# A hybrid of convolution, attention and scan: ScalarE's instructions of the first stage in program order, relus and scaled rows dealt out over the next attention, weight factors moved to the products

## Chip, cores and metric

The kernel runs on one core of one Trainium2 chip, as one program. The metric is the device time of one execution in microseconds (us), as the median of several runs. The engines are called PE (TensorE), ACT (ScalarE), DVE (VectorE), POOL (GpSimd) and SP (SyncE, whose queue issues the DMAs). All data is in 32-bit floats.

## What is computed

The input is x of 4 images, 128 channels, 64 x 64 pixels. Layer 0 is a normalisation by groups and a hybrid of three convolutions and an attention over all pixels; layer 1, over the same data as 4 x 4096 tokens, is a two-way scan (Mamba, heads of 64, chunks of 64) and a recurrent network. The change touches layer 0 alone.

```python
def hybrid(x):                       # layer 0, on v = _gn(input); input + hybrid(v)
    x7 = conv2d(x, w7, b7, 3)        # 7x7, 128 -> 128 channels
    x5 = conv2d(x, w5, b5, 2)
    x3 = conv2d(x, w3, b3, 1)
    theta, phi, g = conv1x1(x, ...)  # 64 channels each, hw = 4096 pixels
    attn = softmax(einsum('bcn,bcm->bnm', theta, phi) / sqrt(64))
    xn = conv1x1(einsum('bcm,bnm->bcn', g, attn), ow, ob) + x
    return relu(x7 + x5 + x3 + xn + x)
# layer 1, on tokens t of layer 0's output
t = t + mamba_forward(_ln_t(t)) + mamba_backward(_ln_t(t))
t = t + recurrent(_ln_t(t))
```

## The kernel before

The function `conv_attention` is the first stage, up to about 1745 us of the profiled span; the second stage (scan and recurrent network) follows. The three convolutions and the residual are one 7x7 convolution, whose weights are added up on the chip (`weights`). It is done by a fast algorithm in both directions: along a row each three taps become two-point forms (`forms`: sums and differences of neighbouring pixels, L325, into tiles `yf`, with one set of weights for sums, one for differences), and down the rows the seven taps of an image's rows split into eight parts m = 0 to 7, at the points 0, plus and minus U = 0.75, plus and minus V = 1.5, and the rest. `transform(m)` (L291 to L310) combines rows of the padded image `xp` into `yx` (with `yb` for help) for m below 6; m = 1, 2 and m = 3, 4 are pairs that share `yb` and the first tile's products. For parts 0 to 5 there are three groups of products (n = 0, 1, 2), for 6 and 7 two. The weights of parts 0 to 5 are made once, at the start, and stored in DRAM as `wd`, three for each part; each group loads its own (`wt<-wd`, 2 buffers, L364), while the middle weights stay in `wc`.

One step n = 8 b + q (32 in all) has an attention and then one part of a convolution of image b. The attention of step n is over 512 queries of the image against its 4096 keys, in eight turns. A turn issues the scores of the next two key tiles (`scores`: four matmuls L421 into a pf tile, two pf tiles of PSUM, then one exp L423 of 128 x 1024 each into one of four `ex` buffers) and then the values of the present two (`values`: L432 on PE, and on DVE the running sum of exponentials `es`, L436 for the first and L438 for the others). After the eighth turn comes `convolve`, one part in the order

```python
ORDER = (1, 2, 0, 6, 7, 5, 3, 4)   # images 0 to 2
LAST = (1, 2, 3, 4, 6, 7, 5, 0)    # image 3
```

Each group of products goes through PSUM tiles `pm` (L351) to `eo`: ACT copies one half (L369), DVE makes sum and difference (L371) and adds the outer products (L374), POOL adds the base of group 0 (L380). Then the results go into the image rows of `t`: for m = 2 by POOL (L386, L387) and three scaled rows on ACT (L388 to L390); for m = 4 by POOL's u and four-row updates on DVE (L398); otherwise by POOL (L403). The matmul `den` (L442) sums es over the partitions, between the groups of products. In the first step of the next image, `finish(b)` goes over the image before in eight parts: load of the untouched input as `xr` (L459, 2 buffers), relu with bias on ACT (L461), addition on POOL (L462). At the last step of an image the convolution is interleaved with the keys of the next (`keys`, L263 to L276), and three steps before its end DVE takes the next image's statistics (`bn_stats`). At the end of each convolution but the last, `queries` (L410, L412) makes the theta of the next step.

The order on PE is the program's (`manual_schedule`); on ACT, DVE, POOL and SP the framework's scheduler orders instructions by its own cost estimates. Each engine runs its instructions strictly in the order that results. The making of weights is spread over steps 0, 1 and 2: `thirds` (from L494), `pair(1)`, `single(0)`, `single(5)`, `pair(3)`, with ACT, DVE and POOL taking part and rows of 128 x 1152.

Of the kernel before, what the change touches and what calls it, by code (L numbers as in the profile page):

```python
# [10 lines left out]
F32 = mybir.dt.float32  # L11
AF = mybir.ActivationFunctionType
ALU = mybir.AluOpType
# [3 lines left out]
P = 128  # L17
# [136 lines left out]
def conv_attention(nc, tc, k, a, t, B, H, W, flags, load, mem, loads):  # L154
# [18 lines left out]
    NQ = T // NC  # L173
    RW = NC // W
    XT = 2 * NC
    KB, PC = H // 4, W // 2
# [5 lines left out]
    U, V = 0.75, 1.5  # L182
    UU, VV = U * U, V * V

    with ExitStack() as ctx:
        wp = ctx.enter_context(tc.tile_pool(name="l0_w", bufs=1))
        wc = wp.tile([P, 9, P], F32, name="wc")
# [10 lines left out]
        yx = wp.tile([P, KB + 1, WP], F32, name="yx")  # L198
        yb = wp.tile([P, KB + 1, WP], F32, name="yb")
        yd = wp.tile([P, KB, WP], F32, name="yd")  # L200
# [27 lines left out]
        ctx.enter_context(tc.manual_schedule(engines={mybir.EngineType.PE}))  # L228
# [58 lines left out]
        def every(j, n):  # L287

            return xp[:, j : j + 4 * n - 3 : 4, :]

        def transform(m):  # L291

            row = lambda j: every(j, KB + 1)
            if m in (0, 5):
                j = m // 5
                nc.scalar.mul(yx, row(j + 2), -(UU + VV))
                nc.scalar.mul(yb, row(j), UU * VV)
                nc.gpsimd.tensor_tensor(yx, yx, row(j + 4), ALU.add)
                nc.gpsimd.tensor_tensor(yx, yx, yb, ALU.add)
            elif m in (1, 3):  # L300
                nc.scalar.mul(yb, row(1), -(VV if m == 1 else UU))
                nc.gpsimd.tensor_tensor(yb, yb, row(3), ALU.add)
                nc.scalar.mul(yx, row(2), -(VV if m == 1 else UU))
                nc.gpsimd.tensor_tensor(yx, yx, row(4), ALU.add)
                nc.scalar.mul(yb, yb, U if m == 1 else V)
                nc.gpsimd.tensor_tensor(yx, yx, yb, ALU.add)
            else:

                nc.scalar.mul(yb, yb, -2.0)
                nc.gpsimd.tensor_tensor(yx, yx, yb, ALU.add)  # L310

        def forms(m):

            def both(rows, g):
                v = rows.rearrange("p (k g) c -> p k g c", g=2)[:, :, g]
                f = fm.tile([P, 4, KB // 2, PC + 2], F32, tag="yf", name="yf", bufs=4)  # L320
                at = lambda j: v[:, :, j : j + 2 * PC + 3 : 2]
                for kx, (x, y, op) in enumerate(
                    ((0, 2, ALU.subtract), (1, 2, ALU.add), (2, 1, ALU.subtract), (3, 1, ALU.subtract))
                ):
                    nc.gpsimd.tensor_tensor(f[:, kx], at(x), at(y), op)  # L325
                return v, f

            if m >= 6:
                return [None] + [[both(every(m - 2, KB), g)] for g in range(2)]
            transform(m)  # L330
            out = [[both(yx[:, 0:KB], 1)]]
            nc.gpsimd.tensor_tensor(yd, yx[:, 0:KB], yx[:, 1 : KB + 1], ALU.subtract)
            for g in range(2):
                out.append([both(yd, g)])
                if m in (0, 5):
                    out[-1].append(both(every(3 + 3 * m // 5, KB), g))
            return out
# [16 lines left out]
        def convolve(b, m, f):  # L354
# [3 lines left out]
            for n in range(3):  # L358
# [10 lines left out]
                nc.scalar.copy(eo[:, 1, :], pm[:, 1, :])  # L369
                for e, op in enumerate((ALU.add, ALU.subtract)):  # L370
                    nc.vector.tensor_tensor(eo[:, e, :], pm[:, 0, :], eo[:, 1, :], op)  # L371
                yield
                pm = products(fn, (0, 3))
                nc.vector.tensor_tensor(eo, eo, pm, ALU.add)  # L374
# [10 lines left out]
                elif m == 2:  # L385
                    nc.gpsimd.tensor_tensor(out(0), in_(mid[n]), in_(eo), ALU.add)  # L386
                    nc.gpsimd.tensor_tensor(mid[n], mid[n], eo, ALU.subtract)  # L387
                    nc.scalar.mul(out(2), out(0), UU)  # L388
                    nc.scalar.mul(out(1), in_(mid[n]), U)
                    nc.scalar.mul(out(3), in_(mid[n]), U * UU)  # L390
# [65 lines left out]
        def finish(b):  # L456
            for q in range(NQ):
                xr = wk.tile([P, NC], F32, tag="xr", name="xr")
                nc.sync.dma_start(xr, image_in(b)[:, bass.ts(q, NC)])  # L459
                r = t[:, ds(b * T + q * NC, NC)]  # L460
                nc.scalar.activation(r, r, AF.Relu, bias=bsum)  # L461
                nc.gpsimd.tensor_tensor(r, r, xr, ALU.add)  # L462

# [16 lines left out]
        def weights():  # L480
# [13 lines left out]
            def thirds(g, new):  # L494

                ac = free[:, 0 : new.shape[1], :]
                nc.gpsimd.tensor_tensor(ac, g[0], g[2], ALU.add)
                nc.scalar.mul(g[1], g[1], 0.5)
                nc.vector.scalar_tensor_tensor(new, ac, 0.5, g[1], ALU.mult, ALU.subtract)
                nc.vector.scalar_tensor_tensor(g[1], ac, 0.5, g[1], ALU.mult, ALU.add)  # L500
# [3 lines left out]
            nc.scalar.copy(wc, w[:, 3])  # L504
            slot = [free[:, bass.ts(i, 9), :] for i in range(3)] + [w[:, 3]]
            one, two = w[:, 0:3], w[:, 4:7]

            def pair(m, at, by):

                first, second = (fm.tile([P, 9, P], F32, tag="wt", name="ws") for _ in range(2))  # L510
                odd = slot[0]
                made = []
                for g, e, s, f in ((one, slot[1], by, slot[2]), (two, slot[3], -by, first)):
                    nc.scalar.mul(odd, g[:, 1], s * at)
                    nc.scalar.mul(e, g[:, 2], s * at * at)
                    nc.vector.scalar_tensor_tensor(e, g[:, 0], s, e, ALU.mult, ALU.add)
                    nc.gpsimd.tensor_tensor(f, e, odd, ALU.add)
                    nc.gpsimd.tensor_tensor(e, e, odd, ALU.subtract)
                    made.append((f, e))
                for i, v in enumerate((odd, second)):  # L520
                    nc.gpsimd.tensor_tensor(v, made[0][i], made[1][i], ALU.subtract)
                    for n, v in enumerate((v, made[0][i], made[1][i])):
                        nc.sync.dma_start(wd[3 * (m + i) + n], v)

            def single(m, i, by):
                v = slot[2], slot[1], slot[0]
                nc.scalar.mul(v[0], one[:, i], by)
                nc.scalar.mul(v[1], two[:, i], -by)
                nc.gpsimd.tensor_tensor(v[2], v[0], v[1], ALU.subtract)
                for n in range(3):  # L530
                    nc.sync.dma_start(wd[3 * m + n], v[n - 1])

            pair(1, U, 0.5 / (UU * (UU - VV)))
            yield
            single(0, 0, 1.0 / (UU * VV))
            yield
            single(5, 2, 1.0)
            pair(3, V, 0.5 / (VV * (VV - UU)))
# [4 lines left out]
        gn, mid, atts, xl = {}, {}, {}, []  # L543
# [20 lines left out]
        for n in range(N):  # L564
# [7 lines left out]
            f = forms(m)  # L572
# [6 lines left out]
            for i in range(NB):  # L579
                exs = nxt  # L580
                if i + 1 < NB:
                    nxt = scores(th, i + 1)
                values(i, exs, acc, es)
            nc.vector.tensor_tensor(es[:, 0, :], es[:, 0, :], es[:, 1, :], ALU.add)
# [1095 lines left out]
```

## Time and profile before

| | |
|---|---|
| median of 3 runs | 3264.07 us (3260.07 to 3266.51) |
| the profiled execution | 3263.07 us, span 3261.3 us |
| granted TensorE clock, mean | 0.961 |
| PE busy | 2971.3 us, 91% |
| DVE busy | 2143.3 us, 66% |
| ACT busy | 1818.7 us, 56% |
| POOL busy | 1624.1 us, 50% |

Times in the profile are microseconds unless marked ns; L351 is line 351 of the kernel before. The row of slices cuts the span into 40 equal parts, each digit the busy share in tenths. A row of waits has the waiting operation, what released it, the total, how many times and the longest. A row of windows has the stretch and its length, then the busy time and number of instructions of PE, PE's weight loads, DVE, ACT and POOL, then the granted clock, the share of the DMA engines and GB/s. A row in order of time has the start, the length, engine, line and operation, the tiles, and in brackets the idle time of the engine just before and what ended it.

### The profile page before, as it was taken

How to read it: one execution, taken by the hardware profiler on the slowest of the kernel's cores; microseconds unless marked ns; L12 is line 12 of the kernel's file. 1: busy time of each engine (PE TensorE's matmuls, PEld its weight loads, DVE VectorE, ACT ScalarE, POOL GpSimd, SP SyncE). 2: the span in 40 equal slices, each digit the busy share in tenths (PEclk: the TensorE clock that was granted, in tenths of full speed). 3: DMA queues.
4: the chain of work that ended last, by engine and by line, in shares of the span. 5: the costliest groups of instructions: out<-in, count | busy, mean ns of one | idle time of the engine just before them, and what ended most of it. 6: DMA issues, size and time to landing. Idle time of an engine off the chain costs nothing. (4 is left out here: it accounts for less than half of the span.)

```text
span 3261.3 us, 42819 instructions
## 1 busy us (share of the span) xinstructions
PE 2971.3 (91%) x15511; PEld 1471.5 (45%) x15511; DVE 2143.3 (66%) x3450; ACT 1818.7 (56%) x3093; POOL 1624.1 (50%) x1352
## 2 busy tenths in 40 slices
PE   5879998899988999899898899999999999999986
PEld 1434544354434435343444354444444444545445
DVE  5666576566765666666665576777676767777767
ACT  3424344433434343434332677887788778888756
POOL 6443436452556415554425256455655565565554
PEclk8889999999999999999998899999999999999988
DMA  3330001000011001110002233333333343333332
GB/s 128 119 128 15 22 30 63 22 22 15 29 45 47 23 0 44 41 44 22 22 15 91 78 92 117 94 93 91 110 93 100 83 113 91 102 99 93 93 112 105
DMA packets 108392, 224.13 MB, mean 69 GB/s; under 512 B 25678, under 2 KB 29390, under 8 KB 106764
## 3 DMA queue, kind: packets, MB, share of 16 engines
q1 hardware_dynamic: 106956, 220.01, 22.5%
q8 instruction: 124, 2.03, 0.2%
q10 hardware_dynamic: 1216, 1.31, 0.1%
q14 instruction: 96, 0.79, 0.1%
HBM read 200.83 MB, written 20.44 MB: 68 GB/s over the span
## 5 line engine op out<-in xcount | busy, mean ns | idle before, releaser
L423 ACT ACTIVATE ex<-pf 128x1024 f32<-128x1024 f32 x512 | 497.7, 1020 | 478.6 <-PE pf L421 444.6
L438 DVE TENSOR_TENSOR es<-es,ex 128x1024 f32<-128x1024 f32 x448 | 607.9, 1357 | 219.5 <-ACT ex L423 190.9
L421 PE MATMUL pf<-theta,phi 64*128 64x512 f32 x2048 | 536.2, 643 | 115.4 <-ACT ex L423 115.4
L432 PE MATMUL acc<-ex,gT 128*64 128x512 f32 x2048 | 501.5, 616 | 0.7 <-ACT ex L423 0.7
L421 PEld LDWEIGHTS pf<-theta,phi 64*128 64x128 f32 x2048 | 179.8, 192 | 444.0 <-ACT ex L423 316.6
L1128 POOL TENSOR_TENSOR ct<-ct,Cst 128x512 f32<-128x512 f32 x128 | 168.8, 1319 | 400.4 <-DMA ct<-csmem 340.8
L1094 ACT ACTIVATE lt<-lt,cs 128x128 f32<-128x128 f32 x1024 | 312.1, 390 | 0.0
L325 POOL TENSOR_TENSOR yf<-xp 128x272 f32<-128x272 f32 x128 | 101.3, 821 | 398.9 <-PE pm L351 398.9
L432 PEld LDWEIGHTS acc<-ex,gT 128*64 128x64 f32 x2048 | 129.7, 139 | 352.4 <-issue 340.9
L351 PE MATMUL pm<-yf,wt 128*128 128x256 f32 x1152 | 287.8, 382 | 0.1
L351 PEld LDWEIGHTS pm<-yf,wt 128*128 128x128 f32 x1152 | 213.9, 190 | 73.2 <-issue 41.3
L1029 PE MATMUL pb<-tl,wbc_fwd 128*64 128x512 f32 x512 | 238.0, 608 | 3.3 <-DVE xT L1061 3.3
L1029 PE MATMUL pb<-tl,wbc_bwd 128*64 128x512 f32 x512 | 238.5, 608 | 0.0
L325 POOL TENSOR_TENSOR yf<-yd 128x272 f32<-128x272 f32 x192 | 189.5, 1015 | 13.0 <-PE pm L351 12.6
L371 DVE TENSOR_TENSOR eo<-pm,eo 128x256 f32<-128x256 f32 x176 | 73.8, 419 | 179.1 <-ACT eo L369 176.9
L1193 POOL TENSOR_TENSOR yT<-yT,zT 128x512 f32<-128x512 f32 x127 | 166.0, 1316 | 35.7 <-DVE yT L1180 32.9
L1127 DVE TENSOR_TENSOR lt<-lt,gm 128x1024 f32<-128x1024 f32 x128 | 181.8, 1420 | 1.9
L369 ACT COPY eo<-pm 128x256 f32<-128x256 f32 x88 | 32.3, 367 | 250.2 <-PE pm L351 250.2
L1061 DVE SCALAR_TENSOR_TENSOR xT<-px,taps_bwd,xT 128x512 f32<-128x512 f32 x192 | 143.8, 749 | 8.1 <-ACT xT L1055 3.3
L1160 PE MATMUL y<-lt,xdt 128*64 128x128 f32 x2048 | 141.9, 281 | 7.6 <-issue 4.2
L1029 PEld LDWEIGHTS pb<-tl,wbc_fwd 128*64 128x64 f32 x512 | 65.9, 139 | 165.8 <-issue 138.7
L1147 POOL TENSOR_TENSOR S<-S,tot 128x256 f32<-128x256 f32 x120 | 93.2, 776 | 92.5 <-PE y L1168 87.8
(301 smaller groups left out, 5643.6 us busy)
## 6 DMA issues: line engine op xcount, KB each, us to landing
lt<-csmem SPq DMA_DIRECT2D x128, 512.0 KB, 5.6
wt<-wd SPq DMA_DIRECT2D x72, 576.0 KB, 3.6
ct<-csmem SPq DMA_DIRECT2D x256, 128.0 KB, 5.2
rs<-m SPq DMA_DIRECT2D x31, 512.0 KB, 3.7
t<-in_x SPq DMA_DIRECT2D x4, 2048.0 KB
rows<-after SPq DMA_DIRECT2D x32, 256.0 KB, 4.7
out<-t SPq DMA_DIRECT2D x4, 2048.0 KB, 14.3
wd<-t SPq DMA_DIRECT2D x14, 576.0 KB, 2.8
```

The lines of the kernel that those rows point to most:

```text
L325: nc.gpsimd.tensor_tensor(f[:, kx], at(x), at(y), op)
L351: nc.tensor.matmul(pm[:, e, :], wt, src, start=(i == 0), stop=(i == len(terms) - 1))
L421: nc.tensor.matmul(pf[:, e, :], phi[HALF[e], m, :], th[HALF[e]], start=True, stop=True)
L423: nc.scalar.activation(ex, pf, AF.Exp, scale=scale)
L432: nc.tensor.matmul(acc[HALF[e]], gT[:, 2 * m + e, :], ex[:, e, :], start=(m == 0), stop=(m == NT // 2 - 1))
L438: nc.vector.tensor_tensor(es, es, ex, ALU.add)
L1029: nc.tensor.matmul(out, w[i]["bc"][:, tap, bass.ts(c, DS)], src, start=(tap == 0), stop=(tap == KC - 1),)
L1061: nc.vector.scalar_tensor_tensor(at(n), px, taps[:, PAD - n : KC - n], at(n), ALU.mult, ALU.add)
L1094: nc.scalar.activation(v, v, AF.Relu, scale=-1.0, bias=m["b"]["cs"][:, d, m["i"], h : h + 1])
L1127: nc.vector.tensor_tensor(lt, lt, gm.unsqueeze(2).to_broadcast([P, ND, NHEAD, P]), ALU.mult)
L1128: nc.gpsimd.tensor_tensor(m["ct"], m["ct"], Cs[:, cols].unsqueeze(1).to_broadcast([P, NHEAD, P]), ALU.mult)
L1193: eng.tensor_tensor(v, v, gr["z"][d][:, :, half(d, j // 2)], ALU.mult)
```

## The change

ACT joins PE in the engines that go in program order. `transform` and `forms` become generators, which are started ahead of the attention and moved on once a turn; for m = 1 and 3 the last addition of the transform comes two turns later. The relu, the load and the addition of `finish` and the three scaled rows of m = 2 go into a list `late`, of which each later turn of an attention takes one off its front, after its scores and values. Factors 0.5 and 0.5 / (e (e - f)) leave the weights: the products are multiplied instead, on the way from PSUM (`BY`; the copy becomes a multiplication, the additions scalar_tensor_tensor). With this the making of weights needs no ACT and fewer instructions; thirds goes by two additions and a subtraction on DVE and POOL, a pair by six rows of DVE and two of POOL, parts 0 and 5 by one addition each and stores straight from the weights. The difference `yd` is taken in two halves. The change leaves the second stage's instructions and their order as they were. Cut to what matters:

```diff
+    BY = {m: 0.5 / (e * (e - f)) for m, e, f in ((1, UU, VV), (2, UU, VV), (3, VV, UU), (4, VV, UU))}
...
         pgb = ps_c.tile([P, 1], F32, tag="c", name="pgb")
         nc.tensor.matmul(pgb, ow[0:IC], gb, start=True, stop=True)
         nc.vector.tensor_tensor(bsum, bsum, pgb, ALU.add)
-        ctx.enter_context(tc.manual_schedule(engines={mybir.EngineType.PE}))
+        ctx.enter_context(tc.manual_schedule(engines={mybir.EngineType.PE, mybir.EngineType.Activation}))
...
         def transform(m):
             row = lambda j: every(j, KB + 1)
-            if m in (0, 5):
-                j = m // 5
-                nc.scalar.mul(yx, row(j + 2), -(UU + VV))
-                nc.scalar.mul(yb, row(j), UU * VV)
-                nc.gpsimd.tensor_tensor(yx, yx, row(j + 4), ALU.add)
-                nc.gpsimd.tensor_tensor(yx, yx, yb, ALU.add)
+            add = lambda v, w: nc.gpsimd.tensor_tensor(v, v, w, ALU.add)
+            if m == 0:
+                nc.scalar.mul(yx, row(2), -(UU + VV) / (UU * VV))
+                nc.scalar.mul(yb, row(4), 1.0 / (UU * VV))
+                add(yx, row(0))
+                add(yx, yb)
+            elif m == 5:
+                nc.scalar.mul(yx, row(3), -(UU + VV))
+                nc.scalar.mul(yb, row(1), UU * VV)
+                add(yx, row(5))
+                add(yx, yb)
             elif m in (1, 3):
                 nc.scalar.mul(yb, row(1), -(VV if m == 1 else UU))
-                nc.gpsimd.tensor_tensor(yb, yb, row(3), ALU.add)
+                add(yb, row(3))
                 nc.scalar.mul(yx, row(2), -(VV if m == 1 else UU))
-                nc.gpsimd.tensor_tensor(yx, yx, row(4), ALU.add)
+                add(yx, row(4))
+                yield
+                yield
                 nc.scalar.mul(yb, yb, U if m == 1 else V)
-                nc.gpsimd.tensor_tensor(yx, yx, yb, ALU.add)
+                add(yx, yb)
             else:
                 nc.scalar.mul(yb, yb, -2.0)
-                nc.gpsimd.tensor_tensor(yx, yx, yb, ALU.add)
-        def forms(m):
+                add(yx, yb)
+        def forms(m, out):
...
                 return v, f
             if m >= 6:
-                return [None] + [[both(every(m - 2, KB), g)] for g in range(2)]
-            transform(m)
-            out = [[both(yx[:, 0:KB], 1)]]
-            nc.gpsimd.tensor_tensor(yd, yx[:, 0:KB], yx[:, 1 : KB + 1], ALU.subtract)
+                out += [None] + [[both(every(m - 2, KB), g)] for g in range(2)]
+                return
+            yield from transform(m)
+            out.append([both(yx[:, 0:KB], 1)])
+            for g in range(2):
+                nc.gpsimd.tensor_tensor(
+                    yd[:, g::2], yx[:, 2 * g : 2 * g + KB - 1 : 2], yx[:, 1:KB:2], ALU.subtract
+                )
             for g in range(2):
                 out.append([both(yd, g)])
                 if m in (0, 5):
                     out[-1].append(both(every(3 + 3 * m // 5, KB), g))
-            return out
         def products(f, kxs):
...
                 pm = products(fn, (1, 2))
                 keep = n and m in (1, 3)
                 eo = wk.tile([P, 2, KB // 2 * PC], F32, tag=f"mid{n}" if keep else "eo", name="eo", bufs=1 if keep else 4)
-                nc.scalar.copy(eo[:, 1, :], pm[:, 1, :])
+                by = BY.get(m, 1.0)
+                nc.scalar.mul(eo[:, 1, :], pm[:, 1, :], by / 2)
                 for e, op in enumerate((ALU.add, ALU.subtract)):
-                    nc.vector.tensor_tensor(eo[:, e, :], pm[:, 0, :], eo[:, 1, :], op)
+                    nc.vector.scalar_tensor_tensor(eo[:, e, :], pm[:, 0, :], by / 2, eo[:, 1, :], ALU.mult, op)
                 yield
                 pm = products(fn, (0, 3))
-                nc.vector.tensor_tensor(eo, eo, pm, ALU.add)
+                if by == 1.0:
+                    nc.vector.tensor_tensor(eo, eo, pm, ALU.add)
+                else:
+                    nc.vector.scalar_tensor_tensor(eo, pm, by, eo, ALU.mult, ALU.add)
                 if n == 0:
                     base = eo
                     yield
...
                 elif m == 2:
                     nc.gpsimd.tensor_tensor(out(0), in_(mid[n]), in_(eo), ALU.add)
                     nc.gpsimd.tensor_tensor(mid[n], mid[n], eo, ALU.subtract)
-                    nc.scalar.mul(out(2), out(0), UU)
-                    nc.scalar.mul(out(1), in_(mid[n]), U)
-                    nc.scalar.mul(out(3), in_(mid[n]), U * UU)
+                    for j, v, by in ((2, out(0), UU), (1, in_(mid[n]), U), (3, in_(mid[n]), U * UU)):
+                        later(nc.scalar.mul, out(j), v, by)
                 elif m == 4:
                     u = wk.tile([P, 2, KB // 2 * PC], F32, tag="u", name="u", bufs=2)
                     nc.gpsimd.tensor_tensor(u, mid[n], eo, ALU.add)
...
             nc.vector.tensor_tensor(r, r, pc, ALU.add)
         def finish(b):
-            for q in range(NQ):
+            def part(q):
                 xr = wk.tile([P, NC], F32, tag="xr", name="xr")
                 nc.sync.dma_start(xr, image_in(b)[:, bass.ts(q, NC)])
                 r = t[:, ds(b * T + q * NC, NC)]
                 nc.scalar.activation(r, r, AF.Relu, bias=bsum)
                 nc.gpsimd.tensor_tensor(r, r, xr, ALU.add)
+            for q in range(NQ):
+                later(part, q)
+        def later(f, *args):
+            late.append(lambda: f(*args))
...
             def thirds(g, new):
                 ac = free[:, 0 : new.shape[1], :]
-                nc.gpsimd.tensor_tensor(ac, g[0], g[2], ALU.add)
-                nc.scalar.mul(g[1], g[1], 0.5)
-                nc.vector.scalar_tensor_tensor(new, ac, 0.5, g[1], ALU.mult, ALU.subtract)
-                nc.vector.scalar_tensor_tensor(g[1], ac, 0.5, g[1], ALU.mult, ALU.add)
+                nc.vector.tensor_tensor(ac, g[0], g[2], ALU.add)
+                nc.gpsimd.tensor_tensor(new, ac, g[1], ALU.subtract)
+                nc.vector.tensor_tensor(g[1], ac, g[1], ALU.add)
             for s in SLOT:
                 thirds([w[:, :, s[i], :] for i in (0, 1, 3)], w[:, :, s[2], :])
-            nc.scalar.copy(wc, w[:, 3])
+            nc.gpsimd.tensor_copy(wc, w[:, 3])
             slot = [free[:, bass.ts(i, 9), :] for i in range(3)] + [w[:, 3]]
-            one, two = w[:, 0:3], w[:, 4:7]
-            def pair(m, at, by):
-                first, second = (fm.tile([P, 9, P], F32, tag="wt", name="ws") for _ in range(2))
-                odd = slot[0]
+            lots = w[:, 0:3], w[:, 4:7]
+            def store(m, both, *own):
+                nc.gpsimd.tensor_tensor(both, *own, ALU.add)
+                for n, v in enumerate((both,) + own):
+                    nc.sync.dma_start(wd[3 * m + n], v)
+            def pair(m, at):
+                spare = [fm.tile([P, 9, P], F32, tag="wt", name="ws") for _ in range(2)]
                 made = []
-                for g, e, s, f in ((one, slot[1], by, slot[2]), (two, slot[3], -by, first)):
-                    nc.scalar.mul(odd, g[:, 1], s * at)
-                    nc.scalar.mul(e, g[:, 2], s * at * at)
-                    nc.vector.scalar_tensor_tensor(e, g[:, 0], s, e, ALU.mult, ALU.add)
-                    nc.gpsimd.tensor_tensor(f, e, odd, ALU.add)
-                    nc.gpsimd.tensor_tensor(e, e, odd, ALU.subtract)
+                for g, e, f in zip(lots, (slot[0], slot[2]), (slot[1], spare[0])):
+                    nc.vector.scalar_tensor_tensor(e, g[:, 2], at * at, g[:, 0], ALU.mult, ALU.add)
+                    nc.vector.scalar_tensor_tensor(f, g[:, 1], at, e, ALU.mult, ALU.add)
+                    nc.vector.scalar_tensor_tensor(e, g[:, 1], -at, e, ALU.mult, ALU.add)
                     made.append((f, e))
-                for i, v in enumerate((odd, second)):
-                    nc.gpsimd.tensor_tensor(v, made[0][i], made[1][i], ALU.subtract)
-                    for n, v in enumerate((v, made[0][i], made[1][i])):
-                        nc.sync.dma_start(wd[3 * (m + i) + n], v)
-            def single(m, i, by):
-                v = slot[2], slot[1], slot[0]
-                nc.scalar.mul(v[0], one[:, i], by)
-                nc.scalar.mul(v[1], two[:, i], -by)
-                nc.gpsimd.tensor_tensor(v[2], v[0], v[1], ALU.subtract)
-                for n in range(3):
-                    nc.sync.dma_start(wd[3 * m + n], v[n - 1])
-            pair(1, U, 0.5 / (UU * (UU - VV)))
+                store(m, slot[3], *(v[0] for v in made))
+                store(m + 1, spare[1], *(v[1] for v in made))
+            pair(1, U)
             yield
-            single(0, 0, 1.0 / (UU * VV))
+            for m, i in ((0, 0), (5, 2)):
+                store(m, slot[i], *(g[:, i] for g in lots))
             yield
-            single(5, 2, 1.0)
-            pair(3, V, 0.5 / (VV * (VV - UU)))
+            pair(3, V)
             yield
         phi = big.tile([P, NT // 2, P], F32, name="phi")
-        gn, mid, atts, xl = {}, {}, {}, []
+        gn, mid, atts, xl, late = {}, {}, {}, [], []
...
             if 3 <= n < B + 2:
                 load(n - 2)
             m = (ORDER if b + 1 < B else LAST)[q]
-            f = forms(m)
+            f = []
+            making_forms = forms(m, f)
+            next(making_forms, None)
             if more:
...
                 if i + 1 < NB:
                     nxt = scores(th, i + 1)
                 values(i, exs, acc, es)
+                next(making_forms, None)
+                if late:
+                    late.pop(0)()
             nc.vector.tensor_tensor(es[:, 0, :], es[:, 0, :], es[:, 1, :], ALU.add)
             for i, _ in enumerate(convolve(b, m, f)):
```

## The prediction

> **What bounds the kernel now.** I read the slices of the span first, then the waits of PE and of ACT over the first stage (0 to 1810 us), then windows that each hold one attention, and last the order of time inside the windows that are too long.
>
> ```profile
> PE   5879998899988999899898899999999999999986
> ACT  3424344433434343434332677887788778888756
> ...
> PE pf L421 <- ACT ex L423: 115.4, 40, 11.6
> ...
> ACT t L388 <- POOL t L386: 35.3, 8, 8.8
> ACT t L461 <- DVE t L398: 27.5, 3, 10.7
> ACT ex L423 <- DVE es L436: 18.5, 2, 13.7
> ```
>
> PE is the engine that sets the end; in the first stage (the first 21 slices) ACT is busy for only a third, and yet PE waits 115.4 us for its exps. The reason is ACT's order: L388 waits for POOL, L461 for DVE, and exps stand behind them. The windows give the price:
>
> ```profile
> 677.89:708.48 30.59, 30.32 (x130) 9.47 (x129) 24.57 (x17) 15.51 (x16) 16.08 (x12) 1.00 0.05 17
> 608.82:651.88 43.06, 33.80 (x130) 10.14 (x129) 21.04 (x19) 19.36 (x23) 19.97 (x20) 0.84 0.04 14
> 39.19:100.73 61.54, 38.88 (x130) 11.71 (x129) 37.23 (x25) 28.59 (x30) 37.56 (x20) 0.75 0.33 124
> 169.09:219.88 50.79, 34.04 (x130) 9.89 (x129) 31.11 (x32) 19.21 (x22) 26.81 (x23) 0.83 0.48 194
> 506.47:546.84 40.37, 32.42 (x130) 10.00 (x129) 32.54 (x26) 19.66 (x23) 27.46 (x20) 0.92 0.18 60
> 1564.46:1607.70 43.24, 32.74 (x130) 10.14 (x129) 30.33 (x31) 15.61 (x16) 16.28 (x14) 0.88 0.04 14
> ```
>
> The first row is an attention at rest: 30.59 us, PE busy for 30.32, granted clock 1.00 (third number from the end). The others are attentions n = 10, 0, 2, 8 and 28. A long one costs twice: PE idles, and the clock is 0.75 to 0.92 afterwards, so that the same 130 matmuls are busy for up to 38.88 us. Measured so, the excess over 30.59 is: n=0 30.9; n=1 6.4; n=2 20.2; n=8, 16, 24 9.8, 12.7, 9.9; n=10, 18, 26 12.5, 12.3, 12.4; n=28 12.7; n=5 and 21 3.4 each; 7, 13, 15, 23 5.5 together. That is 152 us, all that there is to win in attentions; the other sixteen have nothing to give.
>
> What stands ahead of the exps differs, and so does what the change can take away:
>
> ```profile
> 618.15 0.66 ACT L388 ACTIVATE t<-t 128x512 f32<-128x512 f32 x1 [4.07 <-POOL t L386]
> 621.09 1.91 ACT L423 ACTIVATE ex<-pf 128x1024 f32<-128x1024 f32 x2
> 622.14 2.08 PE L421 MATMUL pf<-theta,phi 64*128 64x512 f32 x4 [5.92 <-ACT ex L423]
> ...
> 1579.83 2.51 DVE L398 SCALAR_TENSOR_TENSOR t<-eo,t 128x256 f32<-128x256 f32 x4
> 1582.26 1.21 DVE L436 TENSOR_TENSOR es<-ex 128x1024 f32<-128x1024 f32 x1
> 1583.56 1.94 ACT L423 ACTIVATE ex<-pf 128x1024 f32<-128x1024 f32 x2 [13.74 <-DVE es L436]
> ...
> 66.23 7.20 DVE L438 TENSOR_TENSOR es<-es,ex 128x1024 f32<-128x1024 f32 x2
> 68.86 3.48 POOL L518 TENSOR_TENSOR t<-t 128x1152 f32<-128x1152 f32 x1
> ```
>
> At 618 (n=10) the scaled rows hold ACT. At 1580 (n=28) ACT is free, but its exp waits for a buffer that DVE gives back late, because DVE's own rows L398 stand ahead of the first addition to es. At 66 (n=0) an addition to es takes 3.60 us beside a POOL addition of two SBUF tiles, where it takes 1.21 alone.
>
> **Part by part**, by step of the attention, against the profiled run (3263.07 us, 1.00 below the median of 3264.07).
>
> n=10, 18, 26: each L388 to L390 goes behind one turn's exps, and POOL's L380, L386, L387 of the last products no longer stand behind this part's forms (the 7.8 us of L298, L299 and four L325 between 600 and 608 move into the attention). Nothing is late next but a first es. I take 11.7 of about 12.4 each: **35** (24 to 37).
>
> n=8, 16, 24, 28: the relus leave the path (n=28 has none), but DVE's twelve L398 still wait for POOL's u and still stand ahead of the first es, as in the row at 1579.83; the ring of four ex buffers then stops ACT as it does at 1583.56. Only what POOL does earlier is won: 1 + 3 + 1 + 2.7 = **8** (0 to 20).
>
> n=0, 1, 2: ACT has no weight rows left; DVE gets them. DVE's new order in n=0 has ten es, then a product of the third pair that writes slot[0], which waits until the store of part 0 is out, behind sixteen POOL forms. I place the end of the sums at 109 where it was 104: a loss of **5** (15 lost to 10 gained). n=1 is free of ACT's waits: **6** (2 to 6.4). In n=2 the 24 bn_stats rows and loads stay in DVE's stream; its sum would be ready 48.5 us after the start instead of 60.8: **12** (5 to 18). The conv of n=2 keeps its 6.3 us wait for DVE.
>
> Start: the transform's two muls and three POOL additions leave the keys phase, where PE waited 3.52 us at 38.60; the first score comes 4 us earlier at most: **3.5** (0 to 5).
>
> Convs of n=7, 15, 23: queries wait for ACT, and ACT waits in the transform (L309) for POOL:
>
> ```profile
> PE pt L410 <- ACT g L272: 7.1, 3, 2.4
> ```
>
> With the transform out of the conv: **7** (0 to 7).
>
> Now what the change adds. n=9, 17, 25: each xr load (L459) is put on SP's queue one turn apart and waits for its buffer, which the relu-and-add of two parts earlier frees; the POOL addition comes late, behind the forms (a POOL addition of this shape takes 1.27 to 2.26 us in the trace, a load 2.6). Behind the last of them on SP stands the load of wt for group 2. I get the last load at 43 us after the start, wt at 47.6, needed at 41.5: 6 us of idle time and 1 for the clock in 9 and 17, 2.5 in 25 where the order is kinder: **15** lost (25 to 0).
>
> The transform's muls, 1.20 us each, follow the second exp of an attention, so the third is late: 0.45 us in eleven attentions, **5** lost (10 to 0).
>
> Forms inside the attention: the row at 66.23 gives 3.60 us for an es beside a large POOL addition, and es may take 1.89 (30.59 over 16 with one to spare). Two such additions make es 3.4 us late; the ring allows about 5.3 (four exps of 1.89, less the exp's 1.02 and the es's 1.21). Small POOL rows (L325, 0.62 alone) make an es 1.6, inside 1.89. So I book **5** lost in all (20 to 0). The Trainium skill (SBUF — State Buffer, SBUF: two separate sides) calls it an exclusive lock between GpSimd and a VectorE instruction with two SBUF inputs, where the loser blocks for the whole instruction. The 3.60 us agrees; taken to its end, the rule speaks against this change, for 20 us of es and 17 us of POOL's forms alone would not fit into 30.59 and each attention with a transform would grow by some 6 us (an estimate from this page's rule and the trace's durations). The attention at rest above had 16.08 us of POOL beside 24.57 of DVE and lost nothing, and I go by that row.
>
> Moved factors: the copy L369 becomes a mul (0.37 us either way), L371 and L374 become scalar_tensor_tensor (0.42 for the one; L119's, of a PSUM 128x512, takes 0.69 where L374 takes 0.67). PE waited for none of these in the ordinary convs (idle 0.00): nothing, or 3 lost. The second stage is unchanged: nothing.
>
> Sum: 35 + 8 − 5 + 6 + 12 + 3.5 + 7 − 15 − 5 − 5 = 41.5 us gained. 3263.07 − 41.5 = 3221.6 for a run like the profiled one, 3222.5 by the median.
>
> **Rivals.** *All of it goes.* If DVE, too, comes to its es in time in n=8, 16, 24, 28 (45 us of excess, of which 8 are booked) and xr loads, third exps and es cost nothing, the gain is 41.5 + 37 + 15 + 10 = 103.5: 3160 us. For it: relus and DVE rows wait for the same POOL chain, and POOL is freed of forms. Against: the 13.74 us at 1583.56 had no relu in it.
>
> *The es sums become the bound (slower).* Place: each attention with a transform, 24 of 32. Three additions of 128x1190 (m = 1 and 3) make es 5.1 us late, and if the first es starts another 3.8 late behind DVE's tail, the ring's 5.3 is exceeded by 3.6: 24 × 3.6 = 86 lost against 41.5 won, 3309 us. It decides above (41.5 + 6.5) / 24 = 2.0 us an attention. For it: the row at 66.23, and POOL's busy share of 0.4 to 0.6 moving from convs, where DVE adds little, to attentions, where it adds most. Against: attention n=0 aside, no long es row in the trace stops PE without ACT.
>
> *Nothing is left.* ACT's program order does free the exps, but the new waits (wt behind xr, slot[0], the third exp) and es reach their upper ends, 25 + 15 + 10 + 20 = 70 against 71.5 won: 3262.
>
> **How the numbers follow.** The forecast's case has 0.67, all of it goes 0.08, es bound 0.17, nothing left 0.08. The forecast's own bounds are near 3195 and 3250. The range 3180 to 3272 leaves out most of the first rival and of the second, about 2 in 10. A measurement of this kernel can tell some 0.2%, 6.5 us, from no change. Faster by more: 0.67 + 0.08 and a little of the last case, 0.76; the same: 0.06; slower: 0.18.
>
> **What would show it.** Right: PE's wait for ex falls from 115 to about 50 us; attentions 10, 18, 26 last below 32 us at clock 1.00; 8, 16, 24, 28 still last 37 to 42 with ex waiting for es; the convs of 9 and 17 show PE waiting for a wt load of some 6 us; n=0 still above 60. Wrong: attentions that were at 30.59 now at 33 or more with ACT waiting for es (the second rival); 28 at 31 (the first); or a wait in the convs for eo, DVE's new scalar_tensor_tensor.

## The result, and the profile after

The changed kernel takes 3224.37 us (median of 4 runs, 3221.34 to 3225.97), the kernel before 3263.81 beside it; the ratio is 0.9879 [0.9862, 0.9896]. The forecast was 3222. The profiled execution has a span of 3224.0 us, 37.4 less than before: 35.7 of it lie in the first stage, whose last convolution on PE ends at 1736.25 instead of 1771.96 (the 1745 us of the description above are about the end of its last attention, 1747). The second stage lasts 1487.7 us instead of 1489.4; over all runs below it lasts 1483 to 1492, so that the 1.7 us mean nothing.

The slices of the page, and PE's and ACT's waits over the first stage (total, times, longest):

```profile
PE   5889999899988999899998899999999999999986
...
ACT  3224434333435334343432787887788778888756
POOL 5461757825758446677165266556655664565654
```

```profile
PE pf L437 <- ACT ex L439: 56.8, 40, 17.3
PE pm L364 <- DMA wt<-wd: 23.1, 3, 9.5
PE acc L448 <- ACT ex L439: 13.5, 4, 11.0
PE den L458 <- DVE eo L385: 10.6, 4, 7.5
```

```profile
ACT ex L439 <- DVE es L454: 63.7, 31, 14.2
ACT ex L439 <- DVE es L452: 34.1, 4, 10.5
```

PE waits 57 us for its exps in the scores where it waited 115, and 13.5 us in the values (L448) where it was 0.7; 23 us of a new wait, for weights, have come. ACT's rows of before that waited for POOL and DVE have left the top of its list, and what holds the exps now is DVE: an ex buffer that an addition to es has not yet given back. POOL is busier (56% instead of 50%), because the forms now run beside the additions to es, which slows both: a form's row of 128x272 takes 0.65 us alone and 1.6 there, an es 1.2 alone and 1.5 to 3.5 there.

Windows of six attentions and one convolution (stretch and length, then busy time and instructions of PE, PE's loads, DVE, ACT, POOL; granted clock, DMA share, GB/s):

```profile
659.96:690.55 30.59, 30.32 (x130) 9.47 (x129) 21.82 (x17) 15.51 (x16) 6.61 (x8) 1.00 0.05 18
602.38:633.18 30.80, 30.45 (x130) 9.37 (x129) 25.43 (x15) 21.17 (x24) 29.61 (x17) 1.00 0.06 20
35.57:102.10 66.53, 35.94 (x129) 9.99 (x129) 46.75 (x29) 19.93 (x21) 44.92 (x24) 0.77 0.40 147
165.12:207.08 41.96, 34.30 (x130) 9.65 (x129) 33.68 (x32) 21.32 (x24) 38.24 (x27) 0.92 0.55 221
489.92:529.19 39.27, 33.41 (x130) 10.15 (x129) 34.90 (x26) 18.76 (x19) 32.21 (x18) 0.91 0.05 15
1532.05:1571.50 39.45, 32.14 (x130) 9.94 (x129) 30.34 (x31) 15.62 (x16) 12.00 (x11) 0.91 0.05 16
575.65:602.38 26.73, 18.08 (x68) 14.05 (x68) 11.93 (x22) 1.84 (x4) 14.95 (x12) 0.81 0.38 123
```

The first six are attentions 11, 10, 0, 2, 8 and 28. Attention 10 went from 43.06 to 30.80 us at clock 1.00, with POOL busy for 29.61 of it. There POOL's forms and DVE's additions to es lie side by side:

```profile
608.61 26.81 DVE L454 TENSOR_TENSOR es<-es,ex 128x1024 f32<-128x1024 f32 x14 [1.66 <-ACT ex L439]
...
610.65 3.58 POOL L296 TENSOR_TENSOR yx<-yx,yb 128x1190 f32<-128x1190 f32 x1
614.30 6.28 POOL L335 TENSOR_TENSOR yf<-yx 128x272 f32<-128x272 f32 x4
```

Attention 0 got longer; 8 and 28 are still long. The last row of the seven windows is the convolution of step 9, which took 15.45 us before and lost 11.3. Its row of before:

```profile
593.37:608.82 15.45, 15.45 (x69) 12.34 (x69) 9.20 (x19) 3.82 (x5) 8.49 (x7) 1.00 0.23 76
```

In the changed kernel its matmuls are busy for 18.08 us at clock 0.81, and the rest is a wait, seen in order of time (POOL's additions, SP's loads, PE):

```profile
562.61 11.76 POOL L335 TENSOR_TENSOR yf<-yd 128x272 f32<-128x272 f32 x8
574.33 3.93 POOL L478 TENSOR_TENSOR t<-t,xr 128x512 f32<-128x512 f32 x2
...
576.60 14.32 SPq L475 DMA_DIRECT2D xr<-in_x  x8
590.97 11.83 SPq L377 DMA_DIRECT2D wt<-wd  x3
595.44 5.22 PE L364 MATMUL pm<-yf,wt 128*128 128x256 f32 x12 [8.65 <-DMA wt<-wd]
```

POOL's forms last until 574; only then do its additions free the xr buffers, SP issues the waiting loads until 590.9, and the weights, next in its queue, come 8.65 us too late. In the convolutions of steps 17 and 25 the same wait is 9.5 and 4.9 us.

### The profile page after: what moved, and what is told of

It is laid out like the page before. It is cut to its first block, busy times and chain, and to the rows that moved or that the text cites. A ratio compares the mean times of both kernels' runs of the same rounds, so it can differ in the third digit from the quotient of the medians.

```text
span 3224.0 us, 42883 instructions
## 1 busy us (share of the span) xinstructions
PE 2959.4 (92%) x15511; PEld 1467.2 (46%) x15511; DVE 2279.3 (71%) x3458; ACT 1805.0 (56%) x3078; POOL 1805.3 (56%) x1369
## 5 line engine op out<-in xcount | busy, mean ns | idle before, releaser
L454 DVE TENSOR_TENSOR es<-es,ex 128x1024 f32<-128x1024 f32 x448 | 722.5, 1613 | 117.9 <-ACT ex L439 79.5
L437 PE MATMUL pf<-theta,phi 64*128 64x512 f32 x2048 | 523.2, 629 | 58.2 <-ACT ex L439 56.8
L448 PE MATMUL acc<-ex,gT 128*64 128x512 f32 x2048 | 495.1, 609 | 13.5 <-ACT ex L439 13.5
L383 ACT ACTIVATE eo<-pm 128x256 f32<-128x256 f32 x88 | 33.8, 384 | 481.7 <-PE pm L364 481.7
L448 PEld LDWEIGHTS acc<-ex,gT 128*64 128x64 f32 x2048 | 127.9, 137 | 356.6 <-issue 330.2
L335 POOL TENSOR_TENSOR yf<-yd 128x272 f32<-128x272 f32 x192 | 243.5, 1300 | 0.0
L397 POOL TENSOR_TENSOR eo<-eo 128x512 f32<-128x512 f32 x48 | 62.9, 1310 | 288.3 <-DVE eo L391 220.3
L419 POOL TENSOR_TENSOR t<-t,eo 128x512 f32<-128x512 f32 x32 | 44.0, 1375 | 301.2 <-DVE eo L389 300.0
L385 DVE SCALAR_TENSOR_TENSOR eo<-pm,eo 128x256 f32<-128x256 f32 x176 | 73.5, 418 | 117.4 <-ACT eo L383 115.0
L335 POOL TENSOR_TENSOR yf<-yx 128x272 f32<-128x272 f32 x96 | 148.0, 1570 | 1.9
```

The lines of the kernel that those rows point to most:

```text
L437: nc.tensor.matmul(pf[:, e, :], phi[HALF[e], m, :], th[HALF[e]], start=True, stop=True)
L448: nc.tensor.matmul(acc[HALF[e]], gT[:, 2 * m + e, :], ex[:, e, :], start=(m == 0), stop=(m == NT // 2 - 1))
L454: nc.vector.tensor_tensor(es, es, ex, ALU.add)
```

## Experiments

The times of single runs with a profile (e2, e8, e9) have no interval.

**Program order alone.** e4 is the kernel before with ACT added to `manual_schedule`; e3 is the changed kernel without it.

```diff
e4, on the kernel before:
+        ctx.enter_context(tc.manual_schedule(engines={PE, Activation}))
e3, on the changed kernel:
+        ctx.enter_context(tc.manual_schedule(engines={PE}))
```

> The kernel before with ACT in program order, nothing else (relus stay in the convolution of the next image's first step, scaled rows stay ahead of the first exps of the next attention, the making of weights keeps ACT). My theory: program order alone wins nothing, because the program itself has these rows ahead of the exps: 3262 to 3300, with attentions 10, 18, 26 at 41 to 46 us. Rival: program order alone is the gain: 3220 to 3235.

> The changed kernel with ACT's order left to the scheduler again (PE alone in program order); the list of late rows, the factors and the transform stay as changed. Its order puts the relus and the scaled rows ahead of the first exps again. My theory: program order is what makes the dealing work, so attentions 10, 18, 26 go back to 40 to 43 us and 8, 16, 24 or 9, 17, 25 are long too: 3245 to 3275. Rival: the gain is from lighter weights and earlier POOL work alone, and ACT's order is not needed: 3215 to 3235.

e4: 3264.47 us, ratio to before 1.0004 [0.9992, 1.0017]. Attentions 10, 18 and 26 last 40.6, 40.7 and 41.1 us, 2 shorter than before; attention 2, where the weights' rows on ACT now stand ahead of the exps, lasts 73.5 instead of 50.8. e3: 3290.75, ratio 1.0088 [1.0071, 1.0105], slower than before, and above my range. Attentions 10, 18, 26 last 47.3, 48.2 and 44.4. ACT's order of time in e3's attention 10 shows why:

```profile
611.89 0.67 ACT L485 ACTIVATE t<-t 128x512 f32<-128x512 f32 x1 [6.29 <-POOL t L403]
...
614.82 1.01 ACT L439 ACTIVATE ex<-pf 128x1024 f32<-128x1024 f32 x1
622.64 0.67 ACT L485 ACTIVATE t<-t 128x512 f32<-128x512 f32 x1 [6.82 <-POOL t L403]
```

The scheduler has put the scaled rows back ahead of the exps, as before. So order alone gives nothing in all, dealing without order loses 28 us, and the whole change wins 39. The sums hide that the parts act on different steps. Gained against the profiled run before, in us, up to the end of attention 31 (e5, below, has order and dealing, but the old weights):

| run | start | steps 0 to 2 | steps 3 to 31 |
|---|---|---|---|
| changed kernel | 3.6 | 8.7 | 23.3 |
| e4: order alone | 5.7 | −21.0 | 15.8 |
| e3: dealing and new weights, no order | 0.5 | 10.7 | −38.3 |
| e5: order and dealing, old weights | 6.2 | −13.9 | 25.6 |

The zero of e4 is a loss of 21 where the old weights are made, against as much won elsewhere: order alone shortens attentions 5, 7, 13, 15, 21 and 23 by 9.3 us, as the whole change does. It does not bring 10, 18 and 26 below 40.6; these fall only with order and dealing together.

**The weights.** e5 is the changed kernel with the old `weights()`, the old m = 0 transform and no factors at the products. The second half of yd keeps the changed sign, which the old weights do not make up for, so that group 2's products of parts 0 to 5 enter the output with the other sign; the instructions are the old ones, and one more for yd.

```diff
-                by = BY.get(m, 1.0)
-                nc.scalar.mul(eo[:, 1, :], pm[:, 1, :], by / 2)
+                nc.scalar.copy(eo[:, 1, :], pm[:, 1, :])
...
+                nc.scalar.mul(g[1], g[1], 0.5)          # thirds, pair and single as before
```

> The changed kernel with the weights made as before (ACT, DVE and POOL, factors in the weights) and the products added without factors; program order on ACT, the dealing and the transform stay as changed. My theory: the part of the change that concerns factors is worth what the first three steps show, about 11 us (36.99 to 30.59 in n=1, 50.79 to 41.96 in n=2, 61.54 to 66.53 in n=0), and with ACT's weight rows in program order ahead of the exps it is dearer still: 3232 to 3260, with n=1 and n=2 long and all attentions from n=3 on as in the changed kernel. Rival: the factors moved to the products cost DVE as much in the 28 later steps as they save in three; then 3215 to 3226, with convolutions 6, 14 and 22 back from 17.4 to 15.9.

3245.89 us, ratio 0.9957 [0.9941, 0.9974]: with order and dealing in place, the new weights are worth some 21 us (22.7 in steps 0 to 2 of the profiled runs). That is no share of the 39 by itself: 13.9 of the 22.7 only make good what the old weights lose under ACT's program order. Attention 2 lasts 66.2 us instead of 42.0, attention 0 57.4 instead of 66.5; convolutions 6, 14 and 22 stay at 17.3 to 17.8, so the factors at the products cost nothing that PE sees. All attentions from 3 on are the changed kernel's to within 1 us.

**What holds 8, 16, 24 and 28.** e2 leaves out the loop over L414, the twelve rows of m = 4.

> The changed kernel without the twelve row updates of part m = 4 on DVE (out(1), out(2), out(3) of that part are left out, so the output lacks these terms). My theory: what is left of the long attentions 8, 16, 24 and 28 (38 to 40 us) is that DVE does these rows, which wait for POOL, ahead of the first addition to es. Then all four fall to 30.6 to 31.5 us, and the time by 34 (32 to 36) to about 3190. Rival: POOL's forms or ACT's own rows hold these attentions; then they stay at 36 or more.

3199.42 us. Attention 28 falls to 30.59, 8, 16 and 24 to 32.03 or 32.04; the convolutions behind 8, 16 and 24 take 2.1 us more, of which PE waits 1.8 for es. 25 us came where I expected 34: three attentions keep 1.4 us, and their convolutions give back 2.1 each. DVE's rows ahead of the first es are the cause, as booked. In the changed kernel's attention 28 they read (DVE, ACT):

```profile
1542.48 1.83 DVE L414 SCALAR_TENSOR_TENSOR t<-u,t 128x256 f32<-128x256 f32 x2 [2.72 <-POOL u L409]
1544.23 2.51 DVE L414 SCALAR_TENSOR_TENSOR t<-eo,t 128x256 f32<-128x256 f32 x4
1546.66 1.21 DVE L452 TENSOR_TENSOR es<-ex 128x1024 f32<-128x1024 f32 x1
1547.97 1.94 ACT L439 ACTIVATE ex<-pf 128x1024 f32<-128x1024 f32 x2 [10.55 <-DVE es L452]
```

**The late weights of 9, 17 and 25.** e1 gives xr five buffers, e6 gives wt three.

```diff
e1:
+                xr = wk.tile([P, NC], F32, tag="xr", name="xr", bufs=5)
e6 (and the same for the ws tiles):
+                    wt = fm.tile([P, 9, P], F32, tag="wt", name="wt", bufs=3)
```

> The changed kernel with five buffers for the input loads of the last image (xr) instead of two; nothing else. My theory: the last xr loads stand ahead of the weights of group 2 on SP's queue and wait for buffers that POOL's additions free late, so PE waits 23 us for weights in the convolutions of steps 9, 17 and 25 and its clock falls to 0.81 to 0.85 there. With five buffers only three loads wait, and the weights land in time: those convolutions go from 26.7, 26.5 and 22.4 to 15.0 to 15.9 us, 28 to 31 us in all, time 3193 to 3197. Rival: the weights come late because DRAM or the weight buffer itself is late (the two buffers of wt): then nothing moves, 3224.

> The changed kernel with three buffers for the weights of a group (wt) instead of two, two for xr as changed. In the order that results all weight loads of steps 9, 17 and 25 stand ahead of the xr loads on SP's queue, and ACT's and PE's orders are the same. My theory: the wait is the queue's, so the three convolutions fall to 15.0 to 15.9, by 11.3 + 11.0 + 7.4, 30 us in all: 3192 to 3198. Rival: with five xr buffers 4.9 us of wait were left in step 9 and 6.8 in step 17, so part of it is the transfer itself, beside the xr loads; then 3200 to 3210.

e1: 3213.14 us, ratio 0.9848 [0.9829, 0.9867], a gain of 11 where I expected 28 to 31. The convolutions take 23.2, 23.5 and 15.0: three of eight loads still wait for POOL, and POOL begins its additions only when the forms are done (PE still waits 4.9 and 6.8 us in steps 9 and 17). e6: 3200.31, ratio 0.9816 [0.98, 0.9832]; the convolutions take 15.5, 15.0 and 15.0. The convolution of step 9 in e1, then in e6:

```profile
573.81:597.00 23.19, 18.34 (x69) 14.24 (x69) 11.45 (x22) 1.84 (x4) 14.76 (x12) 0.85 0.43 141
```

```profile
573.87:589.32 15.45, 15.45 (x68) 12.33 (x68) 11.78 (x22) 1.84 (x4) 11.02 (x9) 1.00 0.36 119
```

With three buffers the weights' load stands ahead of the xr loads, which last as long as before (14 us). It is the queue's order, not the transfer: the three convolutions fall by all of their 30 us. The time itself is 24 less than the changed kernel's, 2 outside my range and inside the rival's, because other steps lose a part: attention 26 lasts 35.6 instead of 31.4, the convolutions of 0, 10 and 18 take 2.7, 1.2 and 1.3 more. Why these do is not shown.

**How near the es sums are to being the bound.** e9 doubles the transform's additions on POOL.

```diff
+                nc.gpsimd.tensor_tensor(v, v, w, ALU.add)
+                nc.gpsimd.tensor_tensor(ys, v, w, ALU.add)     # ys is read by nobody
```

> The changed kernel with each large addition of the transform on POOL done a second time into a tile that nobody reads: three more in steps with m = 1 and 3, two with m = 0 and 5, one with m = 2 and 4. It measures how far the es sums are from being the bound. My theory: beside POOL's large addition an es takes 3.6 us instead of 1.9, so six in a row make es 10 us late, the ring of four ex buffers takes 5.3, and attentions with m = 1 and 3 grow by 3 to 6 us, those with m = 0 and 5 (four additions, 6.8 late) by 1 to 2, those with m = 2 and 4 by nothing; convolutions that wait at their start for den grow by 1 to 3 more. In all 20 to 70 us: 3245 to 3295. Rival: POOL's additions do not hold DVE, and nothing but the starts of convolutions whose forms are late changes: 3222 to 3235.

3321.45 us: 97 more than the changed kernel and above my range. Attentions with m = 3 grow by 4.6 (6, 14, 22), with m = 1 by 4.0 to 5.4 (8, 16, 24), with m = 0 by 4.4 (10, 18; I had 1 to 2), with m = 5 by 1.3, with m = 2 and 4 by nothing; and the convolutions grow by 0 to 4, more than I had. In attention 6 of e9 (POOL, DVE):

```profile
401.11 3.50 POOL L298 TENSOR_TENSOR yx<-yx,xp 128x1190 f32<-128x1190 f32 x1
404.57 3.47 POOL L299 TENSOR_TENSOR ys<-yb,xp 128x1190 f32<-128x1190 f32 x1
408.12 3.38 POOL L299 TENSOR_TENSOR ys<-yx,xp 128x1190 f32<-128x1190 f32 x1
...
400.44 30.08 DVE L458 TENSOR_TENSOR es<-es,ex 128x1024 f32<-128x1024 f32 x12 [1.64 <-ACT ex L443]
```

Twelve es take 30.08 us, 2.5 each, where PE's pace leaves 1.9 and the changed kernel's fourteen take 27.45, 2.0 each. The second rival's mechanism is real: two more additions beside es already lengthen an attention by 1.3 to 4.4 us. How many fit before the first microsecond is lost was not measured.

**The first step.** e8 makes the third pair of weights in step 1 and stores parts 0 and 5 in step 2.

> The changed kernel with the third pair of weights made in step 1's place and the stores of parts 0 and 5 in step 2's, nothing else. My theory: in step 0 DVE's product of the third pair waits 11.3 us for the store of part 0 (its target slot[0] is being read out), es behind it; without that store in between the wait goes, attention n=0 falls from 66.5 to 53 to 58 us, and convolution n=2 may wait longer for the weights of part 0, which are then made later: 3208 to 3222. Rival: the wait is DVE's own backlog beside POOL's forms; then n=0 stays over 63.

3218.37 us, in my range for another reason: attention 0 lasts 61.9 (I said 53 to 58), 1 41.6 instead of 30.6 and 2 30.8 instead of 42.0; convolution 1 takes 24.8 instead of 15.0, convolution 2 26.4 instead of 34.8. The wait for the store is gone, but DVE's six products in a row ahead of es remain; only 4.6 of attention 0's excess of 36 went with the store.

**A faster version, in three tries.** e7: wt with three buffers, DVE in program order, its side work dealt out as ACT's.

```diff
+    manual_schedule(engines={PE, Activation, DVE})
+    later(scaled, out(j), in_(v), by)                  # the rows of m = 4
+    if n in (0, 2): next(making)                       # a weight product a turn
+    if b + 1 < B and q == NQ - 4: next(counting)       # a bn_stats a turn
+    if more and i < 4: rows(b + 1, i * H // 4, (i + 1) * H // 4)
```

> A version meant to beat both: the changed kernel with three wt buffers, DVE in program order too, and DVE's side work dealt out over the turns as ACT's was: the twelve rows of m = 4, the weights' additions and products (steps 0 and 2), bn_stats one turn each, the normalised rows in four parts; the four normalised key tiles go ahead of the convolution, and the reductions of a step's divisor behind the next products. My theory: attentions 8, 16, 24 and 28 fall to 30.6 to 33 (28 to 33 us), n=0 from 66.5 to 40 to 50, n=2 from 42 to 31 to 36 and its convolution from 34.8 by 5 to 8, and 30 us come from the weight loads: 3264 to 3224 to about 3105, 3085 to 3135. Rival: es late beside POOL's forms takes the place of the waits, attentions 8, 16, 24 and 28 stay over 36 and others grow: 3150 to 3200.

3213.39 us, ratio 0.9854 [0.9837, 0.987]: 13 slower than e6, 78 above my range and above the rival's as well. Attention 0 falls by 20 us to 46.4, but its convolution takes 33.1 instead of 17.4 and that of step 2 42.7 instead of 34.8 (PE waits 16.2 and 15.6 us in them for weights that are made later now), and the convolutions of 7, 15 and 23 take 4.4 to 7.0 more. Attention 28, without a transform, falls to 30.59 by the dealing; 8, 16 and 24, with one, stay at 38.4. DVE and POOL in attention 8 of e7:

```profile
504.00 6.97 DVE L459 TENSOR_TENSOR es<-es,ex 128x1024 f32<-128x1024 f32 x2
510.89 3.71 DVE L418 SCALAR_TENSOR_TENSOR t<-eo,t 128x256 f32<-128x256 f32 x2
...
506.40 3.49 POOL L300 TENSOR_TENSOR yx<-yx,xp 128x1190 f32<-128x1190 f32 x1
509.96 3.56 POOL L300 TENSOR_TENSOR yx<-yx,yb 128x1190 f32<-128x1190 f32 x1
```

A row of 128x256 takes 0.41 us alone (in attention 28 above the four rows of 2.51 are one of 1.50 beside a POOL addition and three of 0.41); the two rows here take 2.93 and 0.87, and an es 3.5. All twelve rows of attention 8 take 13.4 us where twelve alone would take 4.9. ACT's dealt rows cost nothing (attention 9, with relus dealt over it, lasts 30.59), DVE's take nearly three times their length beside POOL's forms. e10 therefore takes DVE's rows out of attentions with a transform (into the next convolution), and moves the third pair of weights to step 1; e11 adds POOL to program order.

```diff
e10, on e7:
+                if i in (1, 3) and m != 4:
+                    for _ in range(3):
+                        if rest:
+                            scaled(*rest.pop(0))
...
+    if n in (0, 1): next(making)
+    # rows(b + 1, 0, H) after queries(n + 1) of the step before
+    # step 0: three turns' pause in forms after the first form
e11, on e10:
+    manual_schedule(engines={PE, Activation, DVE, Pool})
```

> A second try at a faster version, from the one with DVE in program order (3213): the rows of m = 4 go into the next convolution instead of the next attention, the third pair of weights into step 1's attention instead of step 2's, the normalised rows into the convolution before, and step 0's later forms are issued after its weights. My theory: es additions share with POOL's forms, so DVE's rows do not belong into an attention with a transform: attentions 8, 16 and 24 fall from 38.4 to 32, the convolutions of 7, 15 and 23 go back to 28.6, n=2 loses its 15.6 us wait for weights: 3213 less 18, 15 and 12, 3150 to 3180. Rival: the rows delay the convolutions of 8, 16 and 24 by as much, and n=1 takes over what n=2 loses: 3190 to 3215.

> The second try with POOL in program order too, nothing else. POOL then stores the first pair of weights ahead of step 0's later forms (twelve rows that take 17 us beside DVE). My theory: the convolution of n=0 waits for its weights 10 to 16 us less, all else as in the second try: 8 to 16 us below it. Rival: POOL's program order delays the forms of other steps and loses as much.

e10: 3174.72 us, ratio 0.9728 [0.9712, 0.9744]; attentions 8, 16 and 24 last 32.0, their convolutions 3.4 to 4.6 more than in the changed kernel, step 2 57.1 in all instead of 76.8 and step 1 61.5 instead of 45.6. e10 is in my range. e11: 3167.70, ratio 0.9711 [0.9695, 0.9727], 7 below e10 where I expected 8 to 16; the convolution of step 0 falls from 32.6 to 25.5 us. This is the best of all, 57 us below the changed kernel. PE's waits in e11:

```profile
PE pf L442 <- ACT ex L444: 28.8, 43, 7.1
PE pm L372 <- DMA wt<-wd: 17.0, 2, 8.6
```

## Why the prediction was right, and where it was not

By steps, in us gained (booked, then measured in the profiled executions):

| step | booked | measured |
|---|---|---|
| attentions 10, 18, 26 | 35 (24 to 37) | 35.9 |
| 8, 16, 24, 28 | 8 (0 to 20) | 10.6 |
| n=0 | −5 (−15 to 10) | −5.0, its convolution −1.1 |
| n=1 | 6 | 6.4 |
| n=2 | 12 (5 to 18) | 8.8, its convolution −0.5 |
| start | 3.5 | 3.6 |
| convolutions 7, 15, 23 | 7 | 5.9 |
| 9, 17, 25: weights behind xr | −15 (−25 to 0) | −30.2 |
| third exp late | −5 | −1.1 |
| es beside forms | −5 (−20 to 0) | −6.5, in convolutions 6, 14, 22, 26 |
| attentions 5, 13, 21, 7, 15, 23 | not booked | 9.3 |
| the other convolutions and attentions | nothing | −0.6 |

Unrounded, the measured terms add up to the first stage's 35.7.

**Right, and shown.** The stalls of 10, 18 and 26 were ACT's order, and it took order and dealing together to end them (e3, e4); the excess of 8, 16, 24 and 28 was mostly not ACT's but DVE's (e2; the first rival needed them at 31 us, and they last 38 to 40), and attention 0 would not gain. In n=0 the sign came out by two waits: the booked one (11.3 us on DVE), which e8 shows to be worth 4.6, and the six products in a row ahead of es, which PE waited 17.3 us for and which the prediction does not name.

**The term that was mis-sized: the weights behind xr**, −30.2 against −15, beyond its own bound of −25. I had the last xr load at 43 us after the start of the attention, the weights landed at 47.6 and needed at 41.5. In step 9 they were needed at 41.7, but the last load went out at 45.9, behind POOL's forms, whose twelve rows take 1.5 us each beside es and 0.65 alone; the weights landed at 50.4. So the waits were 8.65, 9.5 and 4.9 us where I had 6, 6 and 2.5. How much of the forms' slowing my 43 held is not written down. The rest is the clock: in step 9 PE's 68 matmuls are busy for 18.08 us in place of 15.45, 2.6 us where I added 1.

**Why the total was nearer than its terms.** Against the 15 us too little stand 9.3 that I left out: the small excesses of 5, 13, 21 and 7, 15, 23, which I had listed among the 152 and then not worked out, and which e4 shows to come with ACT's order alone; and 4 too much for the third exp. That the sum is right to 2 us is luck in these.

**The second rival** did not come true: apart from 0, 2, 8, 16 and 24, which have other causes, the attentions with a transform stay at 30.59 to 30.80 (31.4 to 31.7 in 5, 13, 21 and 26). The measured es tail costs 6.5 us behind attentions with three additions (den waits 1.2 us for es in 6, 14 and 22, and 1.8 in 26, where the view names eo). Its mechanism was well founded: e9 shows attentions growing by 4 to 5 us once the additions double. In attention 10 the single records of the trace alternate: an es and a form's row of 128x272 start in turn, one of each every 1.59 us, where alone they take 1.22 and 0.65. Nearly all of the waiting for each other is thus inside the records, and this is how 29.61 us of POOL and 25.43 of DVE go into 30.80. But a pair takes 0.3 us less than the two alone. The Trainium skill (SBUF — State Buffer, SBUF: two separate sides) has GpSimd and a VectorE instruction with two SBUF inputs shut each other out for a whole instruction. The turns agree with it. The estimate of 6 us an attention, which adds up the lengths alone, does not hold: attention 10 lasts 0.21 more than the 30.59 of an attention at rest. A part of the reason is that a pair takes less than its sum, a part that POOL's last forms run on into the convolution, past 637 where the attention ends at 633.18.

Of the signs named beforehand, PE's wait for ex in the scores fell to 56.8 (I said about 50), the long attentions were those named, and den waited for DVE's new scalar_tensor_tensor for 7.5 us in step 2 (6.3 before, for the addition in its place) and for 0.6, 0.6 and 1.8 in steps 10, 18 and 26, which had no such wait before.

## To carry to other kernels

Dealing side work over a loop's turns worked here only with the engine's order fixed as written: the scheduler put the dealt rows back ahead of the exps. An order fixed as written also keeps what the program has in a bad place, as the old weights showed in e4. Before moving work beside a critical loop, look in the trace for the engines that slow each other there: on ACT the rows were free, on DVE, beside POOL's forms, they took nearly three times their length. And when a load is put on a queue to wait for a buffer, look at what stands behind it; here one more buffer for the load behind was worth more than three for the load that waited.

## What was not expected of the hardware

A wait of 8.65 us cost PE 11.3: the granted clock was 0.81 in that convolution, and the same 68 matmuls were busy for 18.08 us in place of 15.45 at clock 1.00. On DVE, a 128x256 scalar_tensor_tensor took 0.41 us alone and up to 2.93 beside POOL's 128x1190 additions, which themselves took 3.5 where they take 2.5 when nothing delays them.
